# Building the conditional weights of the last 96 batches block by block, 384 columns a pass, between the groups of the shared MLP

## The chip, the core and the metric

The kernel runs on one core of a Trainium2 chip. The time is the device time of one execution in microseconds (us). Engines are named as the profile names them: PE is the matmul engine and PEld its weight loads, DVE the vector engine, ACT the scalar engine, POOL the GpSimd engine, SP the engine that issues most transfers.

## The reference

The input x is 128 batches of 32 tokens of 128 channels, and `cond_8` gives each batch 8 numbers. First comes a conditional layer: each batch has a 128x128 weight matrix of its own, mixed from 8 given matrices with the batch's 8 numbers.

```python
masked_w = weight * mask[None, :, :]
w_bot = jnp.einsum('bg,got->bot', y, masked_w)       # a 128x128 matrix for each of 128 batches
x = x + jnp.einsum('bnt,bot->bno', x, w_bot) + bias
...
w, sel = jax.lax.top_k(softmax(cond_8), 2)           # two experts of eight for each batch
out = sum over experts of we[b] * mlp(x, skill_gate, skill_up, skill_down)
out = out + mlp(x, shared_gate, shared_up, shared_down)
x = x + out                                          # mlp: (gelu(x@gate) * (x@up)) @ down, 128 -> 512 -> 128
```

## The kernel before

All data are float32. Tokens lie as columns, channels as partitions; a tile `t` is 512 columns, that is 16 batches, and there are 8 tiles. The order of work on each engine is the order in which the code issues it, written out by hand.

The conditional weights of a batch (`W[:, b, :]`, 128x128) are built by matmuls that contract over only 32 rows: `wT` holds the masked matrices transposed, in 8 blocks of 16 output channels, and `yd` holds the batches' numbers spread on a diagonal. A matmul uses one of four groups of 32 rows (`j` = 0 to 3), and the four groups write four different PSUM banks. One unit, `make_weights(i, half)`, is 16 matmuls of 128 columns (4 blocks times 4 row groups) for 32 batches and half of the output channels. Its four full banks (128x512) are then copied into `W`: `j` = 0 and 2 by ACT (L289), `j` = 1 and 3 by DVE (L287). All 128 batches take 8 units.

The 8 PSUM banks come from three pools: `ps_g` (2), `ps_u` (3) and `ps_o` (3). `bank()` takes from them in the fixed turn "guouoguo"; the shared MLP takes its own from the same pools. A matmul whose bank is still being read waits for the copy that reads it, and whatever stands behind it in PE's order waits too.

`apply_weights(t)` (L298) multiplies the 16 batches of a tile with their weights, 16 matmuls in groups of 32 columns, into a bank `pz`, which ACT copies to a buffer `z` (L306). `finish_cond(t)` transposes `z` (L315) into a bank `pt`, and DVE adds bias and input into `x1` (L316); for tiles from `EARLY` = 2 on POOL copies `x1` into `acc` (L320).

The routing of batches to experts is a generator of some 70 small DVE instructions; `advance(n)` issues the next `n` steps of it at a chosen place in DVE's order. Two small matmuls on the way count the experts (`ps_n`, L365, copied to `np_sb` at L366) and two give the slots (L538, L539). `Mlp.hidden` of one group is two matmuls of 512 columns, `pg` and `pu` (L575), a GELU on ACT (L580) and a product on DVE (`h`, L582); `down` (L593) adds a group's product into `ps_out`. The shared MLP of a 512-column tile has four groups; `pipe.run` issues a group's `hidden`, then the `down` of the group before it.

The order before, on PE: 3 units (batches 0 to 31, and half of 32 to 63); apply tiles 0 and 1; 2 units; finish 0 and 1; apply 2 and 3; the counts; 2 units; finish 2 and 3; `pg`, `pu` of group 0 of shared tile 0; the last unit; apply 4 to 7; groups 1 and 2; finish 4 to 7; group 3; shared tile 1. Behind that come 27 expert tiles (18 + 4 + 5, with weights loaded by SP as soon as `expert` and `used` are known) and the other shared tiles. A branch for more expert tiles than 27 stands near the end (`tc.If`); it is the only other user of the buffers `h_more`.

Of the kernel before, what the change touches and what calls it, by code (L numbers as in the profile page):

```python
# [10 lines left out]
F32 = mybir.dt.float32  # L11
# [14 lines left out]
EARLY = 2  # L26
# [4 lines left out]
def kernel(  # L31
# [17 lines left out]
    P = 128  # L49
    D, NT = xT.shape  # L50
    B, G = cond.shape
# [3 lines left out]
    TB = 512  # L55
    BT = TB // N
    NTILE = NT // TB
# [15 lines left out]
    const = ctx.enter_context(tc.tile_pool(name="const", bufs=1))  # L73
# [1 line left out]
    ge_pool = ctx.enter_context(tc.tile_pool(name="ge", bufs=3))  # L75
    h_pool = ctx.enter_context(tc.tile_pool(name="h", bufs=4))

    h_more_pool = ctx.enter_context(tc.tile_pool(name="h_more", bufs=4))
    o_pool = ctx.enter_context(tc.tile_pool(name="o", bufs=2))
    w_pool = ctx.enter_context(tc.tile_pool(name="w", bufs=4))  # L80
    xg_pool = ctx.enter_context(tc.tile_pool(name="xg", bufs=3))
# [8 lines left out]
    nc.sync.dma_start(out=cond_sb, in_=cond)  # L90
    mask_sb = const.tile([P, P], F32, name="mask_sb")
    nc.sync.dma_start(out=mask_sb, in_=maskT)
    w0_sb = const.tile([P, G, P], F32, name="w0_sb")
    GQ = 3 * G // 8
    for engine, g in ((nc.sync, slice(0, GQ)), (nc.scalar, slice(GQ, G))):
        engine.dma_start(out=w0_sb[:, g, :], in_=w0T[:, g, :])
    x_sb = []

    def load_x(t, n=1):
# [31 lines left out]
    def warm_up(n):  # L131
# [9 lines left out]
        out=before,  # L141
        in_=ones,
# [40 lines left out]
    OQ = RG // G  # L183
    NJ = P // RG
    OB = OQ * NJ
    NQ = P // OB
    W = const.tile([P, B, P], F32, name="W")
# [25 lines left out]
    yd = const.tile([P, B, OQ], F32, name="yd")  # L213
# [9 lines left out]
    QB = TB // P  # L223
    NB = TB // (QB * OQ)
# [2 lines left out]

    NR = P // OQ
    mw = const.tile([P, NR, G, OQ], F32, name="mw")
    w0_r = w0_sb.rearrange("p g (r o) -> p r g o", o=OQ)  # L230
    mask_r = mask_sb.rearrange("p (r o) -> p r o", o=OQ)
    NRH = NR // 2
    for half in range(2):
        rows = ts(half, NRH)
# [6 lines left out]
    wT = const.tile([P, NQ, P], F32, name="wT")  # L241

    def transpose_weights():
        TQ = QB // 2
        for i in range(NQ // TQ):
            pool, tag = (ps_u, "u") if i % 2 else (ps_g, "g")
            pt = pool.tile([P, TQ * P], F32, name="pt", tag=tag)
            for k in range(TQ):
                q = i * TQ + k
                nc.tensor.transpose(  # L250
                    pt[:, ts(k, P)],
                    mw[:, ts(q, NJ), :, :].rearrange("p j g o -> p (j g o)"),
                    ident,
                )
            copy = nc.vector.tensor_copy if i % 2 else nc.scalar.copy
            copy(wT[:, ts(i, TQ), :].rearrange("p q t -> p (q t)"), pt)
        spread_cond(NB, B - NB)
# [3 lines left out]
    def bank(name):  # L261

        pool, tag = {"g": (ps_g, "g"), "u": (ps_u, "u"), "o": (ps_o, "acc")}[next(ring)]
        return pool.tile([P, TB], F32, name=name, tag=tag)

    def make_weights(i, half):

        banks = [bank(f"w_{j}") for j in range(NJ)]
        q0 = half * QB
        for k in range(QB):  # L270
            for j in range(NJ):
                rows = slice(j * RG, (j + 1) * RG)
                nc.tensor.matmul(  # L273
                    banks[j][:, ts(k, NB * OQ)],
                    wT[rows, q0 + k, :],
                    yd[rows, ts(i, NB), :].rearrange("p b o -> p (b o)"),
                    start=True,
                    stop=True,
                )
        yield  # L280
        for j in range(NJ):
            dst = W[:, ts(i, NB), q0 * OB : (q0 + QB) * OB].rearrange(
                "p b (k o) -> p k b o", k=QB
            )[:, :, :, ts(j, OQ)]
            src = banks[j].rearrange("p (k b o) -> p k b o", k=QB, o=OQ)
            if j % 2:
                nc.vector.tensor_copy(dst, src)  # L287
            else:
                nc.scalar.copy(dst, src)  # L289
        yield  # L290

    def apply_weights(t):

        pz = bank("pz")
        for k in range(TB // P):
            for j in range(P // N):
                b = k * (P // N) + j
                nc.tensor.matmul(  # L298
                    pz[j * N : (j + 1) * N, ts(k, P)],
                    x_sb[t][:, ts(b, N)],  # L300
                    W[:, t * BT + b, :],
                    start=True,
                    stop=True,
                )
        z = h_more_pool.tile([P, TB], F32, name="z", tag="h")
        nc.scalar.copy(z, pz)  # L306
        zs[t] = z

    zs = {}

    def finish_cond(t):
        pt = bank("pt")
        z = zs.pop(t)
        for k in range(TB // P):
            nc.tensor.transpose(pt[:, ts(k, P)], z[:, ts(k, P)], ident)  # L315
        nc.vector.scalar_tensor_tensor(  # L316
            x1[:, ts(t, TB)], pt, bias_sb, x_sb[t], ALU.add, ALU.add
        )
        if t >= EARLY:
            nc.gpsimd.tensor_copy(acc[:, ts(t, TB)], x1[:, ts(t, TB)])  # L320
# [9 lines left out]
    due = []  # L330

    def advance(n):

        for matmuls in due:
            matmuls()
        due.clear()
        for _ in range(n):
            if next(steps, ROUND) is ROUND:
                break
# [211 lines left out]
    steps = routing()  # L551


    class Mlp:


        def __init__(self, n, x_in, weights, finish, widths=None):
            self.n, self.x_in, self.finish = n, x_in, finish
            self.parts = [slice(0, n)]
            if widths:  # L560
                ends = list(itertools.accumulate(widths))
                self.parts = [slice(e - w, e) for w, e in zip(widths, ends)]
            self.wg, self.wu, self.wd = weights
            per_bank = TB // n
            self.groups = [range(c, c + per_bank) for c in range(0, NCH, per_bank)]
            self.ps = None
            self.before_bank = lambda: None
# [83 lines left out]
    pipe = Pipeline(h_pool)  # L651

    def shared_tile(t, widths=None):
        def finish(ps, part):
            w = part.stop - part.start
            cols = slice(t * TB + part.start, t * TB + part.stop)
            if t < EARLY:
                nc.vector.tensor_tensor(acc[:, cols], ps[:, 0:w], x1[:, cols], ALU.add)
            elif t == EARLY:
                nc.vector.tensor_tensor(acc[:, cols], ps[:, 0:w], acc[:, cols], ALU.add)  # L660
            else:
                o = o_pool.tile([P, w], F32, name="o", tag="o")
                nc.vector.tensor_tensor(o, ps[:, 0:w], acc[:, cols], ALU.add)  # L663
                queue = nc.scalar if part.start else nc.sync
                queue.dma_start(out=outT[:, cols], in_=o)

        return Mlp(TB, x1[:, ts(t, TB)], shared, finish, widths)
# [11 lines left out]
    def expert_tile(pipe, kind, i):  # L679
# [40 lines left out]
        def finish(ps, part):  # L720
            for row in rows:
                pipe.parts.append((number, lambda row=row: add(ps, *row)))

        mlp = Mlp(size * N, xg[:, 0 : size * N], weights, finish)

        mlp.before_bank = lambda: pipe.flush(number - 3)
        return mlp


    units = [make_weights(i, half) for i in range(B // NB) for half in range(2)]  # L730

    def weights():
        unit = units.pop(0)
        next(unit)
        next(unit)

    transpose_weights()
    PAIR = NB // BT
    for _ in range(3):
        weights()  # L740
    for i in range(2):
        for t in range(PAIR):
            apply_weights(i * PAIR + t)
        advance(5 if i == 0 else 4)

        for _ in range(2):
            weights()
        for t in range(PAIR):
            finish_cond(i * PAIR + t)

    first = shared_tile(0)
    pipe.run(first, slice(0, 1))
    advance(2)
    weights()
    for t in range(2 * PAIR, NTILE):
        apply_weights(t)
    advance(4)
    pipe.run(first, slice(1, 2))
    advance(5)
    pipe.run(first, slice(2, 3))  # L760
    for t in range(2 * PAIR, NTILE):
        finish_cond(t)

    advance(4)
    pipe.behind = lambda: advance(6)
    pipe.run(first, slice(3, None))
    for t in range(1, EARLY):
        pipe.run(shared_tile(t))
    pipe.behind = lambda: None
    assert not units and not zs and not due and next(steps, None) is None  # L770
    n_used = nc.values_load(
        used[0:1, 0:1],
        min_val=1,
# [4 lines left out]
    others = [(2 - k % 2, k // 2) for k in range(sum(SURE[1:]))]  # L778
# [99 lines left out]
```

## Time and profile before

| | |
|---|---|
| median of 3 runs | 286.03 us (285.97 to 286.47) |
| the profiled execution | 286.84 us, of which the span from the first to the last instruction is 284.9 us |
| PE, share of the span | 278.5 us busy, 98% |
| DVE | 167.1 us, 59% |
| ACT | 78.9 us, 28% |
| POOL | 47.9 us, 17% |
| granted PE clock | 1.00 throughout |
| the matmuls that build `W` (L273) | 256 records, between 7.6 and 25.1 us |
| the slots' matmuls (L538) | start at 46.18 us |

PE's records overlap: a matmul's record runs on past the start of the next, so the distance from one start to the next is what a matmul costs PE. A float32 matmul is two records, two passes over its columns. A gap in PE's row is a gap in its feed. What matters here lies in the first 46 us; from there on the order of work is the same in both kernels.

### The profile page before, as it was taken

What the parts mean: (1) busy time and instruction counts of PE and PEld (TensorE: products, weight loads), DVE (VectorE), ACT (ScalarE), POOL (GpSimd) and SP (SyncE); (2) the same over time, 40 slices, a digit from 0 to 9 for tenths busy, and PEclk for the clock granted to TensorE, in tenths of its full rate; (3) what the DMA queues carried; (4) which work ended last, traced back from release to release, by engine and by line L of the source; (5) the groups of instructions that cost most, each with busy time, mean ns of one, the idle gap of its engine ahead of it and who ended that gap; (6) DMA issues with size and microseconds to landing.
All of it is one profiled execution on the core that took longest, in us unless ns stands there. A gap on an engine that the chain in (4) does not pass through costs nothing. (4 is left out here: it accounts for less than half of the span.)

```text
span 284.9 us, 5162 instructions
## 1 busy us (share of the span) xinstructions
PE 278.5 (98%) x1424; PEld 172.4 (61%) x1424; DVE 167.1 (59%) x487; ACT 78.9 (28%) x149; POOL 47.9 (17%) x285
## 2 busy tenths in 40 slices
PE   7999999999999999999999999999999999999994
PEld 6987544757657567566585665765557444444442
DVE  3889596446666656665566675656666733233232
ACT  4655222222222222222222222222222221222120
POOL 3001032522024211231232222412000000000000
PEclk9999999999999999999999999999999999999999
DMA  6900049433434535335363353333000020100001
GB/s 158 328 9 3 0 112 327 116 92 98 147 112 125 169 103 158 89 98 151 110 183 112 91 171 110 112 115 109 1 2 1 0 110 0 39 37 0 37 37 46
DMA packets 25763, 27.21 MB, mean 96 GB/s; under 512 B 1920, under 2 KB 16768, under 8 KB 25728
## 3 DMA queue, kind: packets, MB, share of 16 engines
q1 hardware_dynamic: 25440, 26.42, 30.6%
q10 hardware_dynamic: 288, 0.39, 0.5%
q8 instruction: 13, 0.21, 0.3%
q14 instruction: 22, 0.18, 0.2%
HBM read 24.71 MB, written 2.10 MB: 94 GB/s over the span
## 5 line engine op out<-in xcount | busy, mean ns | idle before, releaser
L582 DVE TENSOR_TENSOR h<-ge,pu 128x384 f32<-128x384 f32 (+1 forms) x117 | 69.3, 592 | 76.6 <-PE pu L575 76.6
L580 ACT ACTIVATE ge<-pg 128x384 f32<-128x384 f32 (+1 forms) x117 | 61.3, 524 | 186.2 <-PE pg L575 173.6
L711 DVE SCALAR_TENSOR_TENSOR acc<-ps_out,slot_w,acc 128x32 f32 x260 | 65.2, 251 | 27.3 <-DVE h L582 16.8
L593 PE MATMUL ps_out<-h,wd 128*128 128x384 f32 (+2 forms) x216 | 70.3, 425 | 0.0
L575 PE MATMUL pu<-xg,wu 128*128 128x384 f32 (+2 forms) x216 | 70.0, 423 | 0.0
L575 PE MATMUL pg<-xg,wg 128*128 128x384 f32 (+2 forms) x216 | 70.0, 423 | 0.0
L704 POOL COPY xg<-x 128x32 f32 x260 | 41.9, 210 | 120.3 <-PE pu L575 96.4
L575 PEld LDWEIGHTS pg<-xg,wg 128*128 128x128 f32 x216 | 37.7, 190 | 19.8 <-issue 0.7
L593 PEld LDWEIGHTS ps_out<-h,wd 128*128 128x128 f32 x216 | 37.5, 190 | 20.1 <-DVE h L582 1.6
L575 PEld LDWEIGHTS pu<-xg,wu 128*128 128x128 f32 x216 | 37.7, 190 | 19.1
L575 PE MATMUL pg<-x,swg 128*128 128x512 f32 x64 | 32.8, 594 | 0.0
L575 PE MATMUL pu<-x,swu 128*128 128x512 f32 x64 | 32.7, 592 | 0.0
L593 PE MATMUL ps_out<-h,swd 128*128 128x512 f32 (+2 forms) x72 | 32.4, 545 | 0.0
L593 PEld LDWEIGHTS ps_out<-h,swd 128*128 128x128 f32 x72 | 13.3, 190 | 14.9 <-issue 12.2
L575 PEld LDWEIGHTS pu<-x,swu 128*128 128x128 f32 x64 | 12.2, 190 | 15.3 <-issue 15.1
L575 PEld LDWEIGHTS pg<-x,swg 128*128 128x128 f32 x64 | 11.8, 190 | 12.6 <-issue 11.7
L287 DVE COPY W<-w 128x512 f32<-128x512 f32 x16 | 10.0, 683 | 1.0 <-PE w L273 1.0
L273 PE MATMUL w<-yd,wT 32*128 32x128 f32 x256 | 9.5, 281 | 0.4 <-issue 0.4
L273 PEld LDWEIGHTS w<-yd,wT 32*128 32x128 f32 x256 | 8.5, 186 | 1.8 <-issue 1.0
L289 ACT COPY W<-w 128x512 f32<-128x512 f32 x16 | 8.4, 595 | 4.2 <-PE w L273 4.2
L320 POOL COPY acc<-x 128x512 f32<-128x512 f32 x6 | 3.7, 613 | 31.5 <-DVE x L316 31.3
L298 PE MATMUL pz<-W,xin 128*32 128x128 f32 x256 | 7.8, 274 | 0.1
(98 smaller groups left out, 68.5 us busy)
## 6 DMA issues: line engine op xcount, KB each, us to landing
wg<-in_gate_dram SPq DMA_DIRECT2D x27, 256.0 KB, 2.8
wu<-in_up_dram SPq DMA_DIRECT2D x27, 256.0 KB, 3.1
wd<-in_down_dram SPq DMA_DIRECT2D x27, 256.0 KB, 2.9
xin<-in_xT_dram SPq DMA_DIRECT2D x6, 256.0 KB, 5.9
out_dram<-o SPq DMA_DIRECT2D x4, 256.0 KB, 2.0
xin<-in_xT_dram SPq DMA_DIRECT2D x1, 512.0 KB, 7.3
out_dram<-acc SPq DMA_DIRECT2D x1, 512.0 KB, 2.6
w_sb<-in_w0T_dram ACTq DMA_DIRECT2D x1, 320.0 KB, 3.1
```

The source lines that it names most:

```text
L273: nc.tensor.matmul(banks[j][:, ts(k, NB * OQ)], wT[rows, q0 + k, :], yd[rows, ts(i, NB), :].rearrange("p b o -> p (b o)"), start=True, sto ...
L287: nc.vector.tensor_copy(dst, src)
L289: nc.scalar.copy(dst, src)
L298: nc.tensor.matmul(pz[j * N : (j + 1) * N, ts(k, P)], x_sb[t][:, ts(b, N)], W[:, t * BT + b, :], start=True, stop=True,)
L320: nc.gpsimd.tensor_copy(acc[:, ts(t, TB)], x1[:, ts(t, TB)])
L575: nc.tensor.matmul(ps[:, ts(i, self.n)], w[:, ts(c, P)], self.x_in, start=True, stop=True,)
L580: nc.scalar.activation(ge[:, 0:n], pg[:, 0:n], AF.Gelu_apprx_tanh)
L582: nc.vector.tensor_tensor(h[:, 0:n], ge[:, 0:n], pu[:, 0:n], ALU.mult)
L593: nc.tensor.matmul(ps[:, 0 : cols.stop - cols.start], self.wd[:, c, :], h[:, i * self.n + cols.start : i * self.n + cols.stop], start=(c = ...
L704: nc.gpsimd.tensor_copy(xg[:, ts(j, N)], x1[:, bass.ds(v, N)])
L711: nc.vector.scalar_tensor_tensor(a, ps[:, ts(j, N)], slot_w[:, slot0 + j : slot0 + j + 1], a, ALU.mult, ALU.add,)
```

## The change

The first 32 batches are built as before, by two units. The other 96 batches are built together: one call of `weights(32, 96, [q])` makes one block of 16 output channels for all 96 batches, with four matmuls (one for each row group) of 384 columns instead of 128, into four banks of which 384 columns are used, and four copies of 128x384 into `W`. That takes 8 calls in place of 6 units. They are spread out: one before the first two tiles are applied, two behind that, two behind the finish of tiles 0 and 1, two behind `pg`, `pu` of group 0, and one behind group 1. Tiles 2 to 7 are applied together behind group 2, and finished in two lots of three with group 0 of shared tile 1 between them. The steps of the routing are dealt out anew. Four of the six `z` buffers of the later tiles are the space of `w0_sb` and `mw`, which are no longer needed by then, and `h_more` has 2 buffers in place of 4.

```diff
-    h_more_pool = ctx.enter_context(tc.tile_pool(name="h_more", bufs=4))
+    h_more_pool = ctx.enter_context(tc.tile_pool(name="h_more", bufs=2))
...
-    def make_weights(i, half):
+    def weights(b0, n, blocks):
         banks = [bank(f"w_{j}") for j in range(NJ)]
-        q0 = half * QB
-        for k in range(QB):
+        batches = slice(b0, b0 + n)
+        w = n * OQ
+        for k, q in enumerate(blocks):
             for j in range(NJ):
                 rows = slice(j * RG, (j + 1) * RG)
                 nc.tensor.matmul(
-                    banks[j][:, ts(k, NB * OQ)],
-                    wT[rows, q0 + k, :],
-                    yd[rows, ts(i, NB), :].rearrange("p b o -> p (b o)"),
+                    banks[j][:, ts(k, w)],
+                    wT[rows, q, :],
+                    yd[rows, batches, :].rearrange("p b o -> p (b o)"),
                     start=True,
                     stop=True,
                 )
-        yield
         for j in range(NJ):
-            dst = W[:, ts(i, NB), q0 * OB : (q0 + QB) * OB].rearrange(
-                "p b (k o) -> p k b o", k=QB
+            dst = W[:, batches, blocks[0] * OB : (blocks[-1] + 1) * OB].rearrange(
+                "p b (k o) -> p k b o", k=len(blocks)
             )[:, :, :, ts(j, OQ)]
-            src = banks[j].rearrange("p (k b o) -> p k b o", k=QB, o=OQ)
+            src = banks[j][:, 0 : len(blocks) * w].rearrange(
+                "p (k b o) -> p k b o", b=n, o=OQ
+            )
             if j % 2:
                 nc.vector.tensor_copy(dst, src)
             else:
                 nc.scalar.copy(dst, src)
...
-        z = h_more_pool.tile([P, TB], F32, name="z", tag="h")
+        if NB // BT <= t < NTILE - 2:
+            z = (w0_sb if t % 4 > 1 else mw_flat)[:, ts(t % 2, TB)]
+        else:
+            z = h_more_pool.tile([P, TB], F32, name="z", tag="h")
...
+    blocks = iter(range(NQ))
+    def others(n=1):
+        for _ in range(n):
+            weights(NB, B - NB, [next(blocks)])
+    for half in range(2):
+        weights(0, NB, range(half * QB, (half + 1) * QB))
+    others()
+    for t in range(PAIR):
+        apply_weights(t)
+    advance(5)
+    others(2)
+    for t in range(PAIR):
+        finish_cond(t)
+    advance(4)
+    others(2)
     first = shared_tile(0)
     pipe.run(first, slice(0, 1))
     advance(2)
-    weights()
-    for t in range(2 * PAIR, NTILE):
+    others(2)
+    pipe.run(first, slice(1, 2))
+    advance(3)
+    others()
+    pipe.run(first, slice(2, 3))
+    for t in range(PAIR, NTILE):
         apply_weights(t)
-    advance(4)
-    pipe.run(first, slice(1, 2))
-    advance(5)
-    pipe.run(first, slice(2, 3))
-    for t in range(2 * PAIR, NTILE):
+    advance(12)
+    pipe.run(first, slice(3, None))
+    advance(6)
+    second = shared_tile(1)
+    for i, t in enumerate(range(PAIR, NTILE)):
         finish_cond(t)
-
+        if i == (NTILE - PAIR) // 2 - 1:
+            pipe.run(second, slice(0, 1))
     advance(4)
     pipe.behind = lambda: advance(6)
-    pipe.run(first, slice(3, None))
+    pipe.run(second, slice(1, None))
```

More of the change, by code (lines that the diff above doesn't have):

```diff
@@ L92 @@
     nc.sync.dma_start(out=mask_sb, in_=maskT)
-    w0_sb = const.tile([P, G, P], F32, name="w0_sb")
+    w0_sb = const.tile([P, G * P], F32, name="w0_sb")
     GQ = 3 * G // 8
     for engine, g in ((nc.sync, slice(0, GQ)), (nc.scalar, slice(GQ, G))):
-        engine.dma_start(out=w0_sb[:, g, :], in_=w0T[:, g, :])
+        engine.dma_start(
+            out=w0_sb.rearrange("p (g o) -> p g o", g=G)[:, g, :], in_=w0T[:, g, :]
+        )
     x_sb = []
@@ L229 @@
     mw = const.tile([P, NR, G, OQ], F32, name="mw")
-    w0_r = w0_sb.rearrange("p g (r o) -> p r g o", o=OQ)
+    w0_r = w0_sb.rearrange("p (g r o) -> p r g o", g=G, o=OQ)
+    mw_flat = mw.rearrange("p r g o -> p (r g o)")
     mask_r = mask_sb.rearrange("p (r o) -> p r o", o=OQ)
@@ L279, in make_weights @@
                 )
-        yield
         for j in range(NJ):
-            dst = W[:, ts(i, NB), q0 * OB : (q0 + QB) * OB].rearrange(
-                "p b (k o) -> p k b o", k=QB
+            dst = W[:, batches, blocks[0] * OB : (blocks[-1] + 1) * OB].rearrange(
+                "p b (k o) -> p k b o", k=len(blocks)
             )[:, :, :, ts(j, OQ)]
-            src = banks[j].rearrange("p (k b o) -> p k b o", k=QB, o=OQ)
+            src = banks[j][:, 0 : len(blocks) * w].rearrange(
+                "p (k b o) -> p k b o", b=n, o=OQ
+            )
             if j % 2:
@@ L289, in make_weights @@
                 nc.scalar.copy(dst, src)
-        yield
     def apply_weights(t):
@@ L727, in expert_tile @@
         return mlp
[L730 to L735, printed above, removed]
     transpose_weights()
     PAIR = NB // BT
-    for _ in range(3):
-        weights()
[L741 to L749, printed above, removed]
+    blocks = iter(range(NQ))
[13 more added lines that the diff above has]
+    others(2)
     first = shared_tile(0)
@@ L753 @@
     advance(2)
-    weights()
-    for t in range(2 * PAIR, NTILE):
-        apply_weights(t)
-    advance(4)
-    pipe.run(first, slice(1, 2))
-    advance(5)
-    pipe.run(first, slice(2, 3))
-    for t in range(2 * PAIR, NTILE):
+    others(2)
+    pipe.run(first, slice(1, 2))
+    advance(3)
+    others()
+    assert next(blocks, None) is None
+    pipe.run(first, slice(2, 3))
+    for t in range(PAIR, NTILE):
+        apply_weights(t)
+    advance(12)
[3 more added lines that the diff above has]
+    for i, t in enumerate(range(PAIR, NTILE)):
         finish_cond(t)
+        if i == (NTILE - PAIR) // 2 - 1:
+            pipe.run(second, slice(0, 1))
     advance(4)
     pipe.behind = lambda: advance(6)
-    pipe.run(first, slice(3, None))
-    for t in range(1, EARLY):
+    pipe.run(second, slice(1, None))
+    for t in range(2, EARLY):
         pipe.run(shared_tile(t))
     pipe.behind = lambda: None
-    assert not units and not zs and not due and next(steps, None) is None
+    assert not zs and not due and next(steps, None) is None
     n_used = nc.values_load(
```

## The prediction

> **What bounds the kernel now.** I read the page's busy shares and costliest groups first.
>
> ```profile
> PE 278.5 (98%) x1424; PEld 172.4 (61%) x1424; DVE 167.1 (59%) x487; ACT 78.9 (28%) x149; POOL 47.9 (17%) x285
> ...
> L287 DVE COPY W<-w 128x512 f32<-128x512 f32 x16 | 10.0, 683 | 1.0 <-PE w L273 1.0
> L273 PE MATMUL w<-yd,wT 32*128 32x128 f32 x256 | 9.5, 281 | 0.4 <-issue 0.4
> L289 ACT COPY W<-w 128x512 f32<-128x512 f32 x16 | 8.4, 595 | 4.2 <-PE w L273 4.2
> ```
>
> PE is the bound. The chain of waits does not say more (it names the last DVE instruction alone), so I took PE's waits of the first 60 us.
>
> ```profile
> PE warm L133 <- DVE ones L125: 1.1, 1, 1.1
> PE pt L250 <- DVE mw L235: 0.8, 1, 0.8
> PE w L273 <- issue: 0.4, 1, 0.4
> ```
>
> From 11 us on PE waits visibly once, for no engine. So the change is worth what it does to the sum of PE's starts and gaps between 11.43 (first apply) and 46.18 (slots' matmul); behind that both programs are alike. The timeline shows the gap and the pace:
>
> ```profile
> 13.31 1.19 PEld L273 LDWEIGHTS w<-yd,wT 32*128 32x128 f32 x35 [0.20 <-issue]
> ...
> 14.55 1.29 DVE L287 COPY W<-w 128x512 f32<-128x512 f32 x2 [0.45 <-PE w L273]
> 15.09 0.97 PEld L273 LDWEIGHTS w<-yd,wT 32*128 32x128 f32 x29 [0.59 <-issue]
> ```
>
> ```profile
> 19.23 2.07 PE L273 MATMUL w<-yd,wT 32*128 32x128 f32 x64
> ...
> 20.84 2.48 DVE L287 COPY W<-w 128x512 f32<-128x512 f32 x4
> ...
> 23.23 1.40 DVE L316 SCALAR_TENSOR_TENSOR x<-pt,bias_sb,xin 128x512 f32<-128x512 f32 x2
> ...
> 23.97 1.17 PE L273 MATMUL w<-yd,wT 32*128 32x128 f32 x32
> ```
>
> The reader is to see in them: two units from 19.23 to 21.22 (the transposes' start) take 1.99, one unit from 23.97 to 25.07 (apply's start) takes 1.10, so a unit streams in 0.89 and a visit to 32-row matmuls costs 0.21 more, with 0.09 ahead of it (23.45 + 0.43 = 23.88). Full-bank copies on DVE follow each other at 0.60.
>
> **The pace of a 384-column call.** No row shows a 32-row matmul of 384 columns. Eight rounds of four row groups take 0.89, so four groups side by side cost 0.11 a pass, the distance between transposes of 128 columns (8 in 1.09, the last lasting 0.27). The groups run beside each other at full pace.
>
> ```profile
> 52.13 0.81 PE L575 MATMUL pg<-xg,wg 128*128 128x384 f32 x2
> 52.77 0.81 PE L575 MATMUL pu<-xg,wu 128*128 128x384 f32 x2
> ```
>
> Two passes of 384 columns cost 0.64. A call then costs 0.65 if its groups run side by side, 2.6 if one after the other; I take 0.65, the nearest row being the same matmul at 128 columns. The Trainium skill, TensorE: Matmul & The Clock Gate, section "Measured speedup vs the span model", gives 3.07 times, not 4, for four row groups at 512 columns; by it I would estimate 0.85 a call.
>
> Copies of 128x384: DVE's `h` of that width takes 0.55 against 0.68 for a W copy of 512, ACT's GELU 0.49 against 0.60. So I take 0.55 with 0.47 from one to the next on DVE, and 0.48 with 0.38 on ACT (bounds: 0.42, the 128x256 copy of `wT`, and 0.68).
>
> **Up to 13.3 us nothing moves.** Before, the third unit has to wait for the first unit's banks (to 10.13), is done near 11.2, and apply waits for the DVE copy of the second unit that ends at 11.33. The first call waits for the same banks and is done at 10.9; apply starts at 11.43 in both.
>
> **PE's own work after that.** Before: 5 units at 0.89 = 4.46. After: 7 calls at 0.65 = 4.55, as call 1 hid 1/8 where unit 3 hid 1/6: +0.09. Switches between 32-row, 32-column and full matmuls: 4 visits in place of 3 at 0.30 (+0.30), one entry to apply fewer (-0.10), and three exits to `pg` whose first load lies bare (28.88 to 29.84 is 0.96 for two passes, 0.86 for the next two) where before they went to transposes or apply (+0.2): +0.40. The six applies in a row lose the ACT wait at 26.96 (0.24 from start to start in place of 0.06): -0.18.
>
> **The gap at 14.42.** Unit 5 would have streamed from 14.31 to 15.20 and the transposes begun at 15.29; they begin at 16.19: 0.90 lost. The banks it needs were free at 14.03. What fits is the feed of instructions: the page's queue `q8 instruction` moved 13 packets of 0.21 MB, one for about 220 of PE's 2,848 records, and the transfers between 12 and 14 us hold one of them among 202 packets that load x. The changed program issues 48 records fewer in its first call (16 for 64) and 96 fewer in the next visit (32 for 128), and reaches the record number of the gap near 20 us, long after that packet. I take the gap as gone: -0.90 (bounds: -0.90 and 0). The Trainium skill, Runtime: NRT & Kernel Launch, section "Instruction fetch mechanics", says that crossing a block of 16 KiB is mostly hidden; by that rule the gap would be something else and might stay, and the sum would be +2.0.
>
> **The new waits, on banks that DVE frees late.** Calls 2 and 3 run on PE from 13.31 to 14.72 (0.10 for the bare first load, 2 x 0.65), transposes from 14.81 (0.93, from 16.19 to 17.21 less a switch), counts (0.14), call 4 from 15.9, call 5 from 16.7. Before, two applies (1.87) lay between those transposes and the next 32-row matmuls, and DVE caught up under them; that cover is gone. DVE: call 2 is done at 14.23 (13.31 + 0.10 + 0.65, and 0.16 by which a 384-column record outlasts its step), four copies at 0.47 from 14.30, `x1` of tiles 0 and 1 from 16.18 (0.66 each, as in 23.23 to 24.55), `np_sb` at 17.50 to 17.68. Call 5's row groups 1, 2 and 3 take the banks of `pt`, `pt` and `ps_n`, freed by just these three. Group 3 starts at 17.73 in place of 16.7: +1.03. Behind it in PE's order stand `pg`, `pu`.
>
> Then call 5 to 18.38, `pg`, `pu` to 20.29 (0.09 + 0.10 + 4 x 0.43), call 6 at 20.38, call 7 at 21.13. Call 7's second bank is that of `pu`, free when `h` is done. DVE: from `np_sb` to the first copy behind seven routing steps took 1.50 (19.34 to 20.84), so four copies from 19.00, `h` from 20.88 to 21.56: call 7 goes on at 21.61: +0.48. Group 1's `pg` takes the bank of call 7's first row group, which is done at 21.94 and emptied by ACT 0.6 later, near 22.55; PE wants it at 21.61 + 0.65 + 0.09 = 22.35: +0.20. Together +1.71. Without all three, DVE's lateness costs nothing.
>
> Further on no wait is seen: call 8 needs banks freed by 24.2, apply needs the last W copy (near 27.5) at 28.9. At the end of the routing DVE's `both_hot` and PE arrive at the slots' matmul within 0.1 of each other, so that cover is used up. SP's first expert loads come some 6 us earlier, since `expert` does (37.9 before), and POOL's `acc` copies end near 45: the first gather starts at 47.7, both hidden. The smaller `h_more` is not used: 27 expert loads are the sure ones, so the branch is not taken. The `z` buffers cost nothing.
>
> **Sum:** 0.09 + 0.40 - 0.18 - 0.90 + 1.71 = +1.12 us. It is worked out in the profiled execution (286.84, of which 284.9 is span), which is 0.8 above the median of the runs; I add it to the median: 286.03 + 1.12 = 287.15, say 287.2. A measurement can tell some 0.2%, 0.57 us.
>
> **The rivals.**
> 1. The gap at 14.42 goes on, elsewhere in the stream, or is not there in a run without the profiler (the 0.8 between profile and median would allow it): 286.03 + 2.02 = 288.1. For it: nothing names the gap's cause but its count. Against: fewer records in the same time.
> 2. Row groups hinder each other at 384 columns, so that each pass shows its bare load (0.10, as at 28.88): 0.2 a call, partly under the DVE waits, at most 7 x 0.2 = 1.4: up to 288.6. Against: the 0.11 a pass. One after the other (2.6 a call) would be +13; I give that next to nothing.
> 3. Faster: DVE frees the banks in time. Call 5 then starts whole at 16.7, which needs `np_sb` 1.0 earlier in a DVE chain of 3.4 us; from there the sum falls to -0.59, 285.4, and no less. It decides only if W copies of 384 cost about 0.3 apart, far under the 0.42 row.
> 4. The change does only part of this: copies somewhat quicker, waits of about 0.9, within 0.2%: 286.4.
>
> **How the numbers follow.** Forecast 0.55 (286.7 to 287.7), rival 1 0.23, rival 2 0.07, rival 4 0.11, rival 3 0.04. The range takes in the forecast, rival 1 and the upper part of rival 4: 286.6 to 288.4. Slower by over 0.2% (above 286.6) takes the first three and a part of rival 4: 0.88; within 0.2% 0.08; faster 0.04.
>
> **What would show it.** Right: PE's waits after name L316 and L366 (in the changed kernel's numbering) before a `w` matmul near 17, about 1.0 us, and `h` near 21.6; no gap "issue" in 13 to 16; slots' matmul near 47.3. Wrong: that matmul before 46.2; a call much longer than 0.65; a gap "issue" of some 0.5 elsewhere in the first 40 us.

## The result, and the profile after

The changed kernel takes 287.84 us (median of 6 runs, 287.46 to 288.26) where the kernel before took 285.94 beside it: ratio 1.0062 [1.0047, 1.0077], slower by 1.8 us by the ratio. The forecast was 287.2 in 286.6 to 288.4. The profiled execution took 287.99 us, 286.1 of it span.

The page, busy time and costliest groups (busy us, mean ns | idle before it):

```profile
PE 279.8 (98%) x1296; PEld 170.2 (59%) x1296; DVE 167.2 (58%) x491; ACT 79.1 (28%) x153; POOL 47.9 (17%) x285
...
L277 PE MATMUL w<-yd,wT 32*128 32x384 f32 (+1 forms) x128 | 10.8, 401 | 0.0
L292 DVE COPY W<-w 128x384 f32<-128x384 f32 (+1 forms) x20 | 10.3, 575 | 0.7 <-PE w L277 0.7
L294 ACT COPY W<-w 128x384 f32<-128x384 f32 (+1 forms) x20 | 8.7, 514 | 5.7 <-PE w L277 5.7
```

Half as many matmul records build W (128 for 256), and PE is busy as long as before. PE's waits of the first 60 us (sum, times, longest) show little that is new. The gap named issue is gone. The first apply now waits visibly for its last part of W, which costs nothing (from the first W matmul to the first apply it is 3.82 us in both kernels, so up to there nothing moved, as predicted). Of the banks there is only the second line:

```profile
PE pz L302 <- ACT W L294: 0.3, 1, 0.3
PE pg L582 <- ACT W L294: 0.2, 1, 0.2
```

The other waits on banks hide: a 384-column record lasts 0.48 us and more where its step is 0.32, and its end covers them. PE's starts have to be read in the timeline (start, length), and the weight loads' rows, which name in brackets what was waited for:

```profile
12.97 1.67 PE L277 MATMUL w<-yd,wT 32*128 32x384 f32 x16
14.57 1.09 PE L322 MATMUL pt<-ident,z 128*128 128x128 f32 x8
...
15.62 2.64 PE L277 MATMUL w<-yd,wT 32*128 32x384 f32 x16
18.19 1.13 PE L582 MATMUL pg<-x,swg 128*128 128x512 f32 x2
...
20.11 2.03 PE L277 MATMUL w<-yd,wT 32*128 32x384 f32 x16
22.35 1.12 PE L582 MATMUL pg<-x,swg 128*128 128x512 f32 x2 [0.21 <-ACT W L294]
```

```profile
17.27 0.37 PEld L277 LDWEIGHTS w<-yd,wT 32*128 32x128 f32 x4 [0.37 <-DVE x L323]
...
21.21 0.31 PEld L277 LDWEIGHTS w<-yd,wT 32*128 32x128 f32 x6 [0.17 <-DVE h L589]
...
47.45 0.10 PEld L545 LDWEIGHTS <-batch_h 128*128 128x128 bf16 x1 [0.96 <-DVE both_hot L537]
```

DVE's rows for the first of these waits, the two `x1` and the copy of `ps_n`:

```profile
15.82 1.40 DVE L323 SCALAR_TENSOR_TENSOR x<-pt,bias_sb,xin 128x512 f32<-128x512 f32 x2
17.14 0.16 DVE L373 COPY np_sb<-ps_n 128x16 f32<-128x16 f32 x1
```

The last two row groups of call 5 start at 17.27 and 17.35, right behind the second `x1` (17.22) and the copy (17.30). Two calls without a wait (12.97) take 1.60 to the next kind of matmul; the two behind the transposes take 2.57, those behind `pu` 2.24. And the slots' matmul waits for `both_hot`: 0.96 in the load queue, of which 0.30 is lost (46.73 to 47.46 from the start before it, against 0.43 in the kernel before).

The first apply starts at 10.5 to 11.5 us (11.43 and 10.97 in two executions of the kernel before, 11.08 and 11.53 of the changed one; 12.88 in one experiment), and the span ends 3.9 to 4.5 us behind the last matmul. From the slots' matmul to the last matmul all fourteen profiled executions take 234.64 to 234.78. So one execution's span says less than one interval, **first apply to slots' matmul**:

| kernel | interval | median, ratio to the kernel before |
|---|---|---|
| before, two executions | 34.75, 34.09 | 285.94 beside the first runs; 286.18 to 286.41 later |
| after, two executions | 36.38, 36.38 | 287.84, 1.0062 [1.0047, 1.0077]; 287.98, 1.0059 [1.0040, 1.0078] |
| before, x from the third tile on late | 34.73 | 286.40, 0.9973 [0.9949, 0.9998] |
| before, x from the fifth tile on late | 33.87 | 285.55, 0.9983 [0.9970, 0.9996] |
| before, more x traffic | 34.44 | 286.90, 1.0033 [1.0008, 1.0058] |
| after, last six steps earlier | 36.35 | 287.73, 1.0032 [1.0008, 1.0057] |
| after, 16 steps for 12 | 36.07 | 287.76, 1.0070 [1.0044, 1.0095] |
| after, two copies on ACT | 36.07 | 287.67, 1.0038 [1.0014, 1.0062] |
| after, 16 steps and two copies on ACT | 35.76 | 287.39, 1.0037 [1.0022, 1.0052] |
| after, 16 steps, four copies left out | 35.74 | 289.58, 1.0125 [1.0101, 1.0149] |
| after's order, old units | 36.12 | 288.10, 1.0080 [1.0047, 1.0113] |
| after, x from the fifth tile on late | 36.39 | 287.45, 1.0050 [1.0034, 1.0067] |

Two versions with the same interval, 36.07, have ratios of 1.0070 and 1.0038. So a ratio does not rank versions that are 0.3 us apart; the interval does.

### The profile page after: what moved, and what is told of

Read it like the earlier page. It is cut to its first block, busy times and chain, and to the rows that moved or that the text cites. A ratio compares the mean times of both kernels' runs of the same rounds, so it can differ in the third digit from the quotient of the medians.

```text
span 286.1 us, 4914 instructions
## 1 busy us (share of the span) xinstructions
PE 279.8 (98%) x1296; PEld 170.2 (59%) x1296; DVE 167.2 (58%) x491; ACT 79.1 (28%) x153; POOL 47.9 (17%) x285
## 5 line engine op out<-in xcount | busy, mean ns | idle before, releaser
L582 PEld LDWEIGHTS pg<-x,swg 128*128 128x128 f32 x64 | 11.5, 190 | 13.1 <-issue 10.5
L277 PE MATMUL w<-yd,wT 32*128 32x384 f32 (+1 forms) x128 | 10.8, 401 | 0.0
L292 DVE COPY W<-w 128x384 f32<-128x384 f32 (+1 forms) x20 | 10.3, 575 | 0.7 <-PE w L277 0.7
L294 ACT COPY W<-w 128x384 f32<-128x384 f32 (+1 forms) x20 | 8.7, 514 | 5.7 <-PE w L277 5.7
L277 PEld LDWEIGHTS w<-yd,wT 32*128 32x128 f32 x128 | 6.3, 185 | 3.3 <-issue 1.9
L302 PEld LDWEIGHTS pz<-W,xin 128*32 128x32 f32 x256 | 6.9, 110 | 1.7 <-ACT W L294 0.9
```

The lines of the kernel that those rows point to most:

```text
L277: nc.tensor.matmul(banks[j][:, ts(k, w)], wT[rows, q, :], yd[rows, batches, :].rearrange("p b o -> p (b o)"), start=True, stop=True,)
L302: nc.tensor.matmul(pz[j * N : (j + 1) * N, ts(k, P)], x_sb[t][:, ts(b, N)], W[:, t * BT + b, :], start=True, stop=True,)
L582: nc.tensor.matmul(ps[:, ts(i, self.n)], w[:, ts(c, P)], self.x_in, start=True, stop=True,)
```

## The experiments

**The gap at 14.42: the kernel before once more.** No edit.

> The kernel before once more, unchanged. My theory (the gap at 14.42 belongs to a place in PE's stream, where an instruction packet arrives late): the gap of about 0.9 us with the name issue lies at the same matmul again, between the 449th and the 460th PE record, and the slots' matmul follows the first apply by 34.6 to 34.9 us. Rival (a chance event of one profiled execution): no gap of over 0.3 us there, 33.9 us from first apply to slots' matmul. The second use of this run: how much the start, up to the first apply at 11.43, differs between two executions of one program (0.35 between the two profiles).

```profile
12.86 2.27 PE L273 MATMUL w<-yd,wT 32*128 32x128 f32 x64
15.05 1.09 PE L315 MATMUL pt<-ident,z 128*128 128x128 f32 x8
```

The same two units take 2.19 us from start to transposes, where they took 2.88 (13.31 to 16.19). The unhindered two from 18.10 take 2.00 here. So the gap was 0.89 in the one execution that the prediction read, and 0.2 in this one. Both theories were too simple: the place is the same (the 36th matmul of the visit starts 0.67 late there; here the matmuls from the 35th on lose the 0.2 in small steps), the size is not.

**x later, so that nothing is in flight.**

```diff
-    for t in range(EARLY, NTILE - 2):
-        load_x(t)
-    load_x(NTILE - 2, 2)
...
+        if behind is not None:                     # in load_x
+            nc.gpsimd.tensor_copy(xt[:, 0:1], behind)
...                                                # behind the third unit
+    for t in range(EARLY, NTILE - 2):
+        load_x(t, 1, W[:, NB, 3 * OQ : 3 * OQ + 1] if t == EARLY else None)
+    load_x(NTILE - 2, 2)
```

> The kernel before, with the loads of x from the third tile on issued later: the first of them waits for a copy that POOL makes of the last column that the third weights unit writes (12.5 us), so that no x packets are in flight when the instruction packet near 12.5 us is fetched. Feed theory: the gap at 14.42 is gone, 33.9 us from first apply to slots' matmul in place of 34.75, and the median is 0.9 lower, 285.0, as the gap is in unprofiled runs too. Rival A (the gap comes from something in PE's own order, at that place): gap and time stay, 285.9. Rival B (the gap is there in profiled runs only): the gap goes from the trace and the median stays at 285.9. Should tile 2 land later than 17.3 us, PE would wait for xin there, and that wait has to be subtracted.

```profile
17.72 1.08 PE L297 MATMUL pz<-W,xin 128*32 128x128 f32 x32 [0.72 <-DMA xin<-in_xT_dram]
```

No gap (two units in 1.99, from 12.91 to 14.90), but the second apply waits for its x, which cost what was gained. The median settles nothing, so the load was moved for the tiles from the fifth on alone (`2 * EARLY` for `EARLY` in the loops and in the condition):

> The kernel before, with the loads of x from the fifth tile on issued behind a POOL copy of the third weights unit's last column (12.5 us), so that no wait for tile 2 arises. Feed theory: no x packets are in flight between some 10.5 and 13.5 us, the stall in unit 5 (0.90 in one profiled execution, 0.2 in the second) is gone, 33.85 us from first apply to slots' matmul, the median falls by the mean of the stall, 0.3 to 0.6, and the times lie closer together. Rival (the stall is chance, not the traffic's): as before, and the median is the same within 0.2.

```profile
12.73 2.07 PE L272 MATMUL w<-yd,wT 32*128 32x128 f32 x64
14.72 1.09 PE L314 MATMUL pt<-ident,z 128*128 128x128 f32 x8
```

33.87 us in the interval, as forecast from the feed theory (33.85), no gap, and the median is 0.49 lower by the ratio. **This version beats both kernels**, the kernel before by 0.17%. Its twelve times span 0.95 us, the 23 of the kernel before beside it 2.5.

**The reverse: more traffic.**

```diff
+    for t in range(EARLY, NTILE):
+        nc.sync.dma_start(out=acc[:, ts(t, TB)], in_=xT[:, t * TB : (t + 1) * TB])
```

> The kernel before with six loads more: x tiles 2 to 7 are loaded a second time, into the accumulator's columns, which are written again later (1.5 MB behind the x loads, so that the transfers go on to about 17.5 us in place of 13.5). Feed theory: the instruction packets of 12 to 17 us all meet traffic; gaps named issue of 0.5 to 1.5 us in all among the 32-row matmuls between 13 and 21, in each execution, median 0.5 to 1.2 above the kernel before. Rival (the stall has nothing to do with the traffic): 0.0 to 0.2, no gap or one as before.

```profile
13.38 1.19 PEld L275 LDWEIGHTS w<-yd,wT 32*128 32x128 f32 x35 [0.20 <-issue]
14.76 0.97 PEld L275 LDWEIGHTS w<-yd,wT 32*128 32x128 f32 x29 [0.19 <-issue]
...
18.89 0.76 PEld L275 LDWEIGHTS w<-yd,wT 32*128 32x128 f32 x24
19.83 1.21 PEld L275 LDWEIGHTS w<-yd,wT 32*128 32x128 f32 x40 [0.17 <-issue]
```

The loads break between the 35th and the 36th, as in the prediction's fence of the kernel before, and at a second place, 24 into the next visit, where no other execution of this order breaks. The interval is 0.57 longer than without any gap (34.44 for 33.87: 0.47 and 0.26 in the two visits, of which the applies behind them give 0.17 back), and the median 0.64 above the kernel before. x traffic lengthens the gap: with it 0.2 to 0.9, without it 0.

The times of the instruction packets, which the trace holds too, say what PE waits for. The break is at the program's 223rd matmul in all three executions with x in flight, the second one here at the 350th; the 127 matmuls between them are, with their loads, 254 records.

| execution | packet ended | matmul came | behind the packet | lost |
|---|---|---|---|---|
| before, first | 13.53 | 223rd, 15.09 | 1.56 | 0.9 |
| before, second | 12.57 | 223rd, 13.96 | 1.39 | 0.2 |
| more x traffic | 13.28 | 223rd, 14.76 | 1.48 | 0.5 |
| more x traffic, next packet | 18.34 | 350th, 19.83 | 1.49 | 0.3 |
| x from the third tile on late | 10.45 | 223rd, 13.92 | 3.47 | 0 |
| x from the fifth tile on late | 11.68 | 223rd, 13.74 | 2.06 | 0 |

Where there is a gap, the matmul comes 1.4 to 1.6 us behind the end of its packet; where the packet ends 2.0 us ahead or more, there is none (before the 350th too: 1.98 in the first execution, 2.03 and more elsewhere). So by these times the late packet is what PE waits for; no row names it, and why a packet serves only 1.4 us behind its end is not shown.

**A control for the gain: the changed kernel with the same late x.**

> The changed kernel with x loaded as late as in the faster variant of the kernel before, from the fifth tile on. A control: feed theory says that the changed kernel has no such stall to lose, as it issues a quarter of the 32-row matmul records per column, so the time stays within 0.2 of the changed kernel. Rival (the gain there came from the start, the weights landing sooner without x behind them): the same 0.5 us is gained here.

The interval is the same to 0.01 us (36.39), as the theory says (the wide calls issue a third of the records per column, 384 columns for 128, and not a quarter). Yet the median fell, 287.45 beside 287.98, by the ratios some 0.26 us of 286, and their intervals overlap. PE's wait for the masked weights is shorter, here and in the changed kernel run beside it:

```profile
PE pt L252 <- DVE mw L237: 0.2, 1, 0.2
```

```profile
PE pt L253 <- DVE mw L238: 0.5, 1, 0.5
```

But this does not show that the late x is the reason. The first product `mw` starts at 4.78 here and at 5.34 in the changed kernel, and at 4.75 to 4.83 in four versions below (18 steps, 16 steps, two copies on ACT, and the last two together) that load x like the changed kernel: the start varies as much without any change to x. So the rival is neither shown nor excluded. What the gap costs on average stays open between 0.2 us (0.49 less 0.26) and 0.8 (without any gap the stretches differ by 36.38 - 33.87 = 2.51, the medians only by 1.7 to 1.9).

**The slots' wait.** First try, and the second:

```diff
-    advance(12)
+    advance(18)
     pipe.run(first, slice(3, None))
-    advance(6)
```

> The changed kernel, with the routing steps that stand behind the last of its MLP groups (6) brought forward to those behind the six applies (12 become 18), where DVE idles. My theory: the slots' matmul waited 0.30 us for both_hot because the DVE chain of steps ended 0.30 after PE got there; now it ends earlier, the wait is gone and the time falls by 0.3, to 287.5. Rival: the steps wait for each other and for POOL or the z copies all the same, or DVE's earlier steps delay the x1 additions that PE's next MLP tile reads: no change or up to +0.5.

```diff
-    advance(12)
+    advance(16)
```

> The changed kernel, with 16 routing steps in place of 12 behind the six applies, so that four steps (reduction to mine, hot, hot_w, pick: 1.6 us of DVE) come ahead of the six x1 additions (4.0 us) and not behind them. My theory now: the 0.30 us before the slots' matmul are DVE's, whose last chain, from mine to both_hot (3.88 us), cannot start before the sixth x1 addition; four steps earlier both_hot ends 1.6 us earlier, 1.3 ahead of PE, and the wait is gone: 36.1 us from first apply to slots' matmul in place of 36.4, 287.5. Rival: the additions come 1.6 later, so PE's groups of the second MLP tile wait for x1: no gain or a loss up to 1 us.

DVE's rows of the first try, then PE's of the second:

```profile
40.93 2.06 DVE L323 SCALAR_TENSOR_TENSOR x<-pt,bias_sb,xin 128x512 f32<-128x512 f32 x3
42.90 0.16 DVE L522 TENSOR_REDUCE mine<-both 128x2 f32<-128x16 f32 x1
```

```profile
45.75 1.02 PE L600 MATMUL ps_out<-h,swd 128*128 128x512 f32 x2
46.61 0.31 PE L545 MATMUL ps_i<-both_hot,batch_h 128*128 128x344 bf16 x1
```

The first try missed: it brought six steps ahead of the tile's last group, but the chain from `mine` on still stood behind the six `x1` additions, and 3.9 us of DVE follow (42.90 to 46.79, the end of `both_hot`). With four steps more ahead of the additions the slots' matmul follows `ps_out` by the normal 0.86 and the interval is 0.31 shorter, as expected. The median of only 4 runs does not show it; the combined version below does.

**The bank waits: two W copies on ACT.**

```diff
-            if j % 2:
+            if j % 2 and not (j == 1 and blocks[0] in (1, 2) and n > NB):
                 nc.vector.tensor_copy(dst, src)
```

> The changed kernel, with the second W copy of calls 2 and 3 on ACT in place of DVE (two copies of 0.47 off the stretch in which DVE never idles, 13.95 to 21.16). My theory (call 5 and call 7 wait for banks because DVE is late, 0.88 and 0.35 us): DVE gets to x1 0.94 earlier, the waits of call 5 for x1 and np_sb and of call 7 for h go; ACT is then 0.8 later and calls 4 and 5 wait for its copies, 0.7 us in all by the copies' 0.41; the sum is 0.3 to 0.5 less than the changed kernel, 287.4. Rival (the wait is not DVE's load but the order, x1 needs the transposes anyway): the waits for x1 stay near 0.9, time the same or, with ACT's delay on top, up to 0.7 more.

The interval fell by 0.30, all of it in the visit behind the transposes (2.25 for 2.57). The visit behind `pu` stays at 2.24, so the wait of call 7 did not get less as I had said. The rest of it is a question to the next run: **four DVE copies left out.**

```diff
+            if j % 2 and n > NB and blocks[0] in (1, 2):
+                continue
             if j % 2:
                 nc.vector.tensor_copy(dst, src)
```

> The kernel of the run with 16 steps, without the DVE half of the W copies of calls 2 and 3 (four copies of 0.47; those parts of W stay at zeros that POOL writes near 3 us, so the result is not the reference's). My theory: all three new bank waits (0.88, 0.35, 0.28) come from DVE's load between 13.95 and 21.16; 1.9 us of it less makes calls 5 and 7 start in time, so 34.6 to 34.9 us from first apply to slots' matmul and about 286.2. What is then left over the kernel before (34.09 in its second profiled execution) is PE's own: 0.09 for the calls and 0.40 for the switches less 0.18. Rival (the waits are the order's: x1 cannot come sooner, as it needs the transposes): call 5 still waits over 0.5, 35.5 us or more.

```profile
17.43 2.09 PE L278 MATMUL w<-yd,wT 32*128 32x384 f32 x16
19.66 1.12 PE L585 MATMUL pg<-x,swg 128*128 128x512 f32 x2
...
21.58 1.84 PE L278 MATMUL w<-yd,wT 32*128 32x384 f32 x16
23.82 1.12 PE L585 MATMUL pg<-x,swg 128*128 128x512 f32 x2 [0.40 <-ACT W L297]
```

```profile
18.53 0.37 PEld L278 LDWEIGHTS w<-yd,wT 32*128 32x128 f32 x4 [0.16 <-DVE x L326]
19.66 0.30 PEld L585 LDWEIGHTS pg<-x,swg 128*128 128x128 f32 x2 [0.76 <-ACT W L297]
```

My theory fell for the larger part. With 1.9 us of DVE taken away the interval is 0.33 shorter than with 16 steps alone, not 1.2 to 1.5. The visit behind the transposes still takes 2.23: `x1` now starts at 17.07, as soon as the transposes allow, and its two additions and `np_sb` end at 18.56 with call 5 waiting; then ACT's copies are the next in line. The visit behind `pu` takes 2.24 as in the changed kernel, though `h` starts 0.11 behind the end of `pu`: the wait for `h` is less, the one for ACT's copies more (0.40 for 0.21), because `pg` takes the bank of call 7's first row group, and ACT has three copies, 0.37 apart, to make between call 6 and there. So in this order, with DVE relieved, the transposes that `x1` needs and ACT's copies are the next to hold the banks; no run relieved ACT too. (The median of this run is not comparable: POOL's fill of W delays the start by some 2 us; see the end.)

**Order or width?** The order of the changed kernel with units of 32 batches and 128 columns, dealt out 1, 1, 2, 1, 1.

```diff
-            weights(NB, B - NB, [next(blocks)])
+            i, half = next(blocks)
+            weights(i * NB, NB, range(half * QB, (half + 1) * QB))
```

> The changed kernel's order with the old units (32 batches, four blocks, 128 columns a pass) in its visits, as 1, 1, 2, 1 and 1 units for the 1, 2, 2, 2 and 1 calls. Theory (the order does it: between the transposes and the next 32-row matmuls no applies are left, and eight PSUM banks turn over too slowly): the second unit behind the transposes waits for x1 and np_sb as call 5 did, 0.7 to 0.9 us, the slots' matmul still waits 0.3, 35.8 to 36.1 us from first apply to slots' matmul, 287.2 to 287.6. Rival (the width does it: a 384-column call fills three quarters of a bank and needs 28 banks where the units needed 20): the waits but the last go, 34.8 to 35.2 us, 286.4 to 286.7.

```profile
14.88 0.77 PE L322 MATMUL pt<-ident,z 128*128 128x128 f32 x5 [0.36 <-issue]
...
19.91 1.17 PE L277 MATMUL w<-yd,wT 32*128 32x128 f32 x32
21.74 1.12 PE L582 MATMUL pg<-x,swg 128*128 128x512 f32 x2 [0.66 <-ACT W L294]
```

It is no faster (36.12; 1.0080), so the narrow passes do not save the order. The waits stand elsewhere than I said: the two units behind the transposes take 2.32 (15.61 to 17.93) for 2.0, probably since a gap named issue (14.88; the transposes take 1.50 for 0.93) let DVE catch up, and the single unit before `pg` 1.83 for 1.10. With the gap taken off whole (0.58) this order would take some 35.5, an estimate, and the same units in the old order take 33.87 without a gap. So the order costs at least some 1.7 us, and the width some 0.3 to 0.8 (36.38 less 36.12 or 35.5); how the gap and the waits trade against each other is not told.

The gap itself bears on the feed: it is again at the program's 223rd matmul, 1.34 us behind the end of its packet (13.54), though that matmul is a transpose here and a 32-row matmul in the kernel before. It goes by the count of instructions, not by their kind. The wide calls reach their 223rd matmul only at 21.64, 9.0 us behind the packet's end.

**Both repairs together.**

> The changed kernel with both repairs that the earlier runs showed: 16 steps behind the applies (the slots' wait, 0.30) and the second W copy of calls 2 and 3 on ACT (0.31). Theory: they add up, 35.8 us from first apply to slots' matmul, 0.5 to 0.6 below the changed kernel. Rival: both act on the same wait, 36.1.

They add up: 35.76, and 287.39 beside 287.98. Still slower than the kernel before, 1.0037 [1.0022, 1.0052].

**The changed kernel once more.**

> The changed kernel once more, unchanged, beside the others on the same chip: every theory expects about 287.8 and 36.4 us from first apply to slots' matmul; how far this interval varies between two executions says how exactly it may be read. No gap with the name issue of over 0.2 us among the 32-row matmuls, if the feed theory is right.

The interval repeats to 0.01 us, with no gap.

## Why the prediction was right

The number lies in the range, above the forecast's own 286.7 to 287.7 and below rival 1's 288.1. The forecast's own span ends 0.14 below it: it is the room made for rival 1 that holds it. In the first pair of executions the interval grew by 1.62 (34.75 to 36.38) where the sum said 1.12. Term by term, PE's own work being the interval less waits, against the 33.87 without a gap:

| step | predicted | measured |
|---|---|---|
| PE's own: pace and switches, less ACT's wait | +0.31 | 36.38 - 1.51 - 0.30 - 33.87 = +0.70 |
| the gap at 14.42 | -0.90 | -0.89 in that execution, -0.2 in the second |
| waits on banks, calls 5, 7 and `pg` | +1.03, +0.48, +0.20 | +0.88, +0.35, +0.28 |
| slots' matmul | 0, "cover used up" | +0.30 |

- **Pace.** 0.65 a call, as taken: 384-column passes of call 2 start at 12.97, 13.39, of call 3 at 13.72, 14.04. The estimate from the Trainium skill (TensorE: Matmul & The Clock Gate, "Measured speedup vs the span model"), 0.85 a call, does not hold here; the measurement decides. Rival 2 is out.
- **Switches** were under-sized. Four visits cost 1.21 beside the calls' 4.55 and the waits, 0.30 each where I took 0.21. The last one, a single call, costs just the 0.21 (25.12 to 25.98); in the three with two calls some row groups start the second call behind the others, with a bare load (records of 0.58 us, not 0.48), and that adds 0.10 to 0.19. And each change between MLP passes and other shapes shows 0.10 on both sides (19.15 to 20.11 is 0.96, not 0.86), which gives +0.50 in the MLP where I put 0.29 (0.20 for the exits to `pg`, 0.09 ahead of one more visit). The applies gave 0.30 back as reckoned (0.28), the transposes 0.15 that I had not reckoned.
- **The gap** was this sum's weak term, and rival 1 held in part. I took one execution's 0.90 for the kernel's; it ranges from 0.2 to 0.9 in two executions, and by the runs averages between 0.2 and 0.8. Its cause, an instruction packet that comes late among x loads, stands up to the experiments on the traffic and to the packets' own times; the two breaks of the run with more traffic lie 127 matmuls apart, 254 records with their loads, where I reckoned 220 to a packet. The Trainium skill (Runtime: NRT & Kernel Launch, "Instruction fetch mechanics") calls such crossings mostly hidden: that agrees with the kernel without x in flight (none shows), not with x in flight.
- **The bank waits** were named rightly, by place, by releaser (`x1` and `np_sb`, L323 and L373 in the changed kernel; the numbers that the prediction gives are the old ones) and to 0.2 in sum (1.51 for 1.71). The reason given, that DVE is late with W copies, holds for a part: taking two or four copies away gives 0.3. What stands behind it, by the run with the old units, is the order: transposes, `x1` and calls share eight banks with no applies between them.
- **The slots' wait**: I saw the two arrive together and priced the tie at nothing. The six `x1` additions in two lots push the last 3.9 us of the routing to the end, and 0.30 came of it.

So the errors cancelled in part: +0.39 and +0.30 too little, 0.20 too much on the waits, 0.1 to 0.7 too much credit for the gap.

## What to carry to other kernels

A wider pass over the same columns saves records, not PE time, where row groups already run side by side: here 7 calls of 0.65 replace 5 units of 0.89, and each extra visit costs switches. Before work is packed closer on the busy engine, follow each PSUM bank: what stood between a bank's fill and its next use was the cover, and taking load off the emptying engine returned little here, as the next emptier was as late. And do not book a gap named issue at the size that one execution shows.

## What the hardware showed unexpectedly

- A stall at one fixed matmul of the program, the 223rd, whatever kind it is. It cost 0.9, 0.2, 0.5 and 0.6 us in four executions in which the instruction packet had ended 1.3 to 1.6 us before, and nothing where the packet ended 2.1 us or more before; in a stream of 32-row matmuls of 128 columns (some 70 matmuls and loads a us), not in the 384-column calls.
- While POOL filled 128x3072 of SBUF (2.97 to 5.63 us), two small DVE instructions between SBUF tiles stood until it ended. In the run with copies left out, and in the one with 16 steps:

```profile
3.59 2.12 DVE L200 COPY cond_rep<-cond_sb 128x128 f32<-128x128 f32 x1 [1.78 <-DMA cond_sb<-in_cond_dram]
```

```profile
3.60 0.23 DVE L199 COPY cond_rep<-cond_sb 128x128 f32<-128x128 f32 x1 [1.80 <-DMA cond_sb<-in_cond_dram]
```

- A bank wait of 0.3 us may appear in no idle time of PE at all, since records overlap; the distance of starts and the load queue's row have it.
